# Moving the ALiBi bias of half of the heads behind exp, onto GpSimd, with a new order of the steps

## The chip, the core and the metric

The kernel runs on one core of a Trainium2 chip. A core has a matrix engine (TensorE, "PE" in the profile, with its weight loads as "PEld"), three engines for elementwise work (VectorE or "DVE", ScalarE or "ACT", GpSimd or "POOL"), and a queue that mostly issues transfers (SyncE, "SP"). Each engine works through its own list of instructions in order and waits for the others through semaphores. The metric is the device time of one execution in microseconds (us): the median over several executions.

## The reference

All data are fp32. The input is four batches of 1024 tokens with 128 features. Two blocks follow one another, and each adds to x the product of an attention and a gated feed-forward net:

```python
xn = layernorm(x);  x = x + attention_0(xn) * silu(ffn_0(xn))
xn = layernorm(x);  x = x + attention_1(xn) * silu(ffn_1(xn))
```

The first attention has 16 heads of 8 features, a causal window of 65 keys and a bias that falls linearly with the distance (ALiBi):

```python
score = q @ k.T / sqrt(128) + slope[head] * (key_pos - query_pos)
score = where((dist >= 0) & (dist <= 64), score, -inf)
out   = softmax(score) @ v
```

The first feed-forward net mixes eight experts' weights into one pair of matrices per batch, by gates that come from the mean over the batch's tokens. The second attention runs over the *batch* axis: each token position is a sequence of four. The second feed-forward net is silu(w1 x) * (w2 x), two square 512 by 512 layers with gelu, and a last projection.

## The kernel before

**Units and slices.** The first attention and all feed-forward work go by units: a unit is 512 tokens of one batch, and there are eight (0 to 7). Within a unit the first attention goes by four tiles of 128 queries (t = 0 to 3). The second attention goes by eight slices of 128 positions over all four batches; slices 0 to 3 need only units 0, 2, 4 and 5, slices 4 to 7 need all.

**The order is written out by hand.** `ORDER` is a list of words, each of them one step, and `program` emits the instructions of each word in that order (line 855). Every engine thus has its part of the list as its queue, and an instruction that waits holds up all that is behind it on its engine. `program` is emitted twice, with `exact` False and True, and a flag that the kernel computes from the weights (line 256) chooses one of them at run time. With these inputs the branch with `exact` False runs. The words that matter here, with u for the unit, t for the tile and b for the batch:

| word | step | engines |
|---|---|---|
| q u, m u g, v u i | queries, keys and values of a unit; copies with masks; copies of v | PE; ACT; DVE (ACT for unit 0) |
| s u t | `scores`: 12 matmuls into a tile `ps_S` of four PSUM banks, of which there is one (line 425) | PE |
| b u t | `biased`: score + bias from PSUM into an SBUF tile `pr` (line 442) | DVE |
| x u t | `power`: exp of `pr`, in place (line 776) | ACT |
| o u t | `weighted`: `pr` times v and a column of ones, so that the sums for the softmax come along (line 473) | PE |
| c, p, d | copy, transpose and divide by the sums | ACT, PE, DVE |
| A, B, C, D, E | gates of a batch and the mixing of experts, E being one of 16 adds (line 351) | PE, ACT, DVE |
| f, g | first net: gelu, then silu (lines 517, 532) | PE, ACT |
| r, l/t, n, k | residual; statistics, scaling and transposing back of a layernorm | POOL; DVE, POOL; DVE; PE, ACT |
| w, h, i, j | second net: gated, two square layers, last projection (lines 564, 576, 589) | PE, ACT, DVE |
| *A to *Y | second attention of one slice (lines 618 to 717): project, gates, products (*b), score (*C), exp (*E), norm (*N), values (*D), sums (*G), turn back (*T), project out (*F), output (*Y) | mostly DVE and POOL |
| y | last tokens of the last batch (line 731) | DVE |

The scores tile has one buffer, so s of the next tile can begin only when its readers are done. `pr` comes from a pool `big` of six tiles of 128x2048, which the nets and the second attention use too; in the first 40 us four of the six hold the experts' weights. The outputs of *Y and y go through `t2k`, a pool of three buffers, and are free again when their transfer has landed. PSUM tiles of one bank take turns over three banks, and `BANKS` writes out which.

**Bias and mask.** The array `bias` has, for each key (partition), head and query, the bias, and -1e30 where the mask forbids the key. It is loaded once (line 170) on ACT's queue, 1 MB. Heads lie in `bias[:, j, g]`, j and g from 0 to 3.

Of the kernel before, what the change touches and what calls it, by code (L numbers as in the profile page):

```python
# [11 lines left out]
AF = mybir.ActivationFunctionType  # L12
ALU = mybir.AluOpType
# [3 lines left out]
P = 128  # L17
# [29 lines left out]
def constants():  # L47
# [30 lines left out]


ORDER = """  # L80
    l1
    q0 m02 m00 m03 m01 A00 n10 s00 k10 b00 A01 B0 L0 s03 b03 C0 D0 E0 E0 E0 E0 v01 s01 b01 E0 H0 v03 E0 v02
    L1 x00 v00 E0 x01 E0 x03 s02 b02 E0 o00 o01 c01 E0 x02 f0 l3 E0 f0 f0 E0 o02 E0 o03 E0 E0 p01 E0 c03
    q1 d01 m13 g0 m12 m11 p03 l2 L2 d03 f0 m10 n20 g0 n30 k20 s10 b10 f1 r0 f1 f1 t0 f1 v12 A10 v13 n01 k30
    s13 b13 k01 A11 B1 w0 s11 v11 w0 w0 C1 l6 w0 b11 n60 x13 v10 x10 x11 h0 l4 g1 k60 s12 o10 n40 o11 c11 D1
    g1 b12 p11 E1 x12 h0 h0 d11 o12 l7 l5 o13 k40 c13 E1 E1 E1 E1 E1
    q2 E1 H1 m23 n50 v20 m21 m22 E1 v21 m20 h0 E1 s20 b20 f3 k50 E1 v23 A20 E1 f3 x20 p13 s22 d13 v22 r1 f2
    b22 t1 A21 x22 B2 i0 n11 n70 E1 E1 i0 s21 o20 b21 k11 x21 i0 C2 i0 D2 s23 o21 w1 b23 c21 w1 E1 w1 o22 w1
    x23 h1 p21 E1 f2 E1 o23 c23 Z f2
    q3 E2 f2 m31 m32 h1 m30 m33 E2 g2 v31 d21 E2 f3 E2 g2 p23 s30 d23 b30 f3 r2 x30 E2 v30 t2 h1 v33 h1 A30  # L90
    s31 E2 n21 v32 k70 j0 b31 x31 j0 E2 A31 o30 o31 E2 E2 c31 s32 f4 i1 b32 x32 s33 k21 b33 E2 x33 i1 f4 g3
    g3 p31 B3 o32 o33 H2 d31 E2 E2 c33 i1
    q4 E2 C3 v41 D3 w2 E3 m40 m41 m43 m42 p33 i1 s40 E3 d33 v40 r3 v43 w2 w2 w2 E3 b40 t3 x40 h2 h2 s41 v42
    E3 n31 h2 E2 b41 x41 h2 s42 o40 o41 k31 E2 z f4 b42 c41 f4 j1 j1 x42 s43 E3 b43 x43 i2 i2 w3 i2 w3 i2
    p41 o42 E2 o43 c43 w3
    q5 d41 v51 m50 w3 p43 m53 h3 g4 E3 m52 m51 g4 E3 h3 d43 h3 E3 v53 h3 s50 v52 b50 x50 i3 s51 f5 v50 i3
    b51 E3 j2 E3 r4 E3 f5 E3 E3 E3 x51 t4 i3 n41 s52 o50 o51 k41 b52 j2 w4 s53 w4 c51 w4 w4 H3 b53 x52 x53
    i3 h4 o52 o53 p51 f6 E3 c53 f6 d51
    q6 E3 f6 f5 p53 m60 f5 d53 f6 v63 j3 g6 v62 g5 v61 m62 g5 r5 t5 m61 j3 g6 n51 h4 h4 m63 k51 h4 s61 *A0
    i4 b61 *A0 s60 v60 w5 *A0 w5 w5 w5 x61 *A0 b60 x60 i4 i4 s62 *B0 *b0 i4 *A1 b62 *C0 h5 *E0 j4 o60 *N0  # L100
    o61 s63 c61 *D0 x62 j4 b63 h5 x63 *A1 h5 o62 o63 *A1 *A1 p61 c63
    q7 m70 d61 m73 p63 d63 v71 *B1 *D0 v72 *b1 m72 *G0 h5 f7 m71 i5 *A2 s70 r6 *A2 i5 b70 v73 x70 *C1 *E1
    v70 s71 *A2 *A2 b71 *N1 x71 i5 i5 *D1 o70 o71 s72 c71 f7 f7 b72 t6 f7 s73 x72 *D1 b73 n61 x73 g7 g7 j5
    p71 *B2 j5 k61 *b2 o72 d71 *G1 o73 c73 *A3 p73 d73 w6 *A3 *A3 r7 *A3 t7 w6 *C2 w6 *B3 *T0 w6 n71 *E2 h6
    *b3 *N2 *C3 k71 *D2 h6 *E3 h6 *N3 *D2 *D3 h6 w7 w7 *A4 *A4 *D3 w7 *A5 *A4 *G3 *A4 *A5 *B4 *A5 *A5 *b4
    *C4 *T3 i6 *B5 *T1 *F0 *E4 *b5 *C5 i6 i6 *E5 i6 *N4 *G2 j6 *Y0 *N5 j6 *D4 w7 *D4 *A6 *A6 *D5 h7 *G4 *A6
    *A6 *T2 *B6 *D5 *A7 *A7 *b6 *A7 h7 *F1 *C6 *E6 *A7 h7 *Y1 *G5 *B7 h7 *N6 *b7 *D6 *T5 i7 *C7 *E7 *D6 *N7
    *T4 *D7 *F5 i7 *G6 i7 *F3 *T6 *F2 *Y5 *F4 *D7 i7 *Y3 *G7 *T7 *Y4 *F6 *Y2 j7 *Y6 *F7 j7 y0 *Y7 y1
"""
# [10 lines left out]
def block_kernel(ctx: ExitStack, tc: tile.TileContext, a: dict, out: bass.AP):  # L122
    nc = tc.nc
    PE, DVE, ACT, POOL = nc.tensor, nc.vector, nc.scalar, nc.gpsimd
# [23 lines left out]
    g1 = main.tile([P, B, S], F32, tag="g1", name="g1")  # L148
# [18 lines left out]
    nc.scalar.dma_start(out=x[:, 0, U:S], in_=a["x"][:, U:S])  # L167
    nc.sync.dma_start(out=vec, in_=a["vec"])
    nc.sync.dma_start(out=wg, in_=a["wg"])
    nc.scalar.dma_start(out=bias.rearrange("p j g q -> p (j g q)"), in_=a["bias"])  # L170
    nc.sync.dma_start(out=tb.rearrange("p c e -> p (c e)"), in_=a["tb"])
    nc.sync.dma_start(out=w1, in_=a["w1"])
    nc.sync.dma_start(out=w2, in_=a["w2"])
# [113 lines left out]
    def program(exact):  # L287
# [8 lines left out]
        def big(shape=(P, 4, 4, P)):  # L296
            return ffn.tile(list(shape), F32, tag="big", name="big", bufs=6)
# [67 lines left out]
        made = {}  # L365
# [73 lines left out]

        def biased(u, t, sp):  # L440
            pr = big()
            DVE.tensor_tensor(pr, sp, bias, ALU.add)  # L442
# [153 lines left out]
        def attend(sl, pool, late):  # L596
# [110 lines left out]
            def gated_out():  # L707
# [63 lines left out]
        def bias_add(u, t):  # L771
            put(("pr", u, t), biased(u, t, made["sp", u, t]))

        def power(u, t):
            pr = made["pr", u, t]
            ACT.activation(pr, pr, AF.Exp)  # L776
# [158 lines left out]
```

## Time and profile before

| | us |
|---|---|
| median of 3 runs (lowest, highest) | 542.19 (541.60, 543.24) |
| the profiled execution | 542.32 |
| its span, first to last instruction | 540.5 |
| PE busy | 521.0 (96%) |
| DVE busy | 348.7 (65%) |
| ACT busy, of it table loads | 344.8 (64%), 127 |
| POOL busy | 119.7 (22%) |

The span and the profiled execution's own time differ by 1.8 us, which lie outside of the instructions. In the profile a matmul in fp32 appears as two instructions. A row of the groups gives the line, engine and operation, the tile written and those read, shapes and count, then the busy time in us and the mean in ns, then the idle time in front of it and what ended it.

### The profile page before, as it was taken

The page shows a single profiled execution, that of the slowest core. Times are in us where ns is not written, and L with a number is a line of the kernel's source. Part 1 is how long each engine was busy: PE and PEld are TensorE (multiplying, and loading weights), DVE is VectorE, ACT ScalarE, POOL GpSimd, SP SyncE. Part 2 cuts the span into 40 slices and gives each one's busy share as a digit, 9 for nine tenths or more (in the row PEclk, how much of TensorE's full clock was granted, in tenths as well). Part 3 has the DMA queues.
Part 4 walks back from the last instruction along what each step waited for, and adds up shares of the span by engine and source line. Part 5 has one row for each costly group of instructions (what it writes and reads, how often), then busy time and mean ns, then how long its engine had stood idle before and what let it go on. Part 6 is the DMA issues. An engine that isn't in the chain of part 4 may idle for free.

```text
span 540.5 us, 10505 instructions
## 1 busy us (share of the span) xinstructions
PE 521.0 (96%) x4448; PEld 293.3 (54%) x4448; DVE 348.7 (65%) x657; ACT 344.8 (64%) x417; POOL 119.7 (22%) x149
## 2 busy tenths in 40 slices
PE   8599999999999999999999999999999999999993
PEld 4266465545665545556455584446545744465453
DVE  6898778934563668114365223546578799888995
ACT  2477686976898766965596643557568565654441
POOL 3023011400210020000110002011142433737653
PEclk9889999999999999999999999999999999999998
DMA  8942005102221112011110000000000000000003
GB/s 318 403 182 99 2 2 158 54 26 79 79 79 41 41 40 79 1 40 39 40 40 2 1 1 0 1 0 3 1 1 3 1 0 1 0 20 2 19 15 108
DMA packets 10726, 27.32 MB, mean 51 GB/s; under 512 B 1040, under 2 KB 5296, under 8 KB 9648
## 3 DMA queue, kind: packets, MB, share of 16 engines
q1 hardware_dynamic: 10240, 25.01, 13.4%
q10 hardware_dynamic: 432, 1.57, 0.8%
q8 instruction: 36, 0.59, 0.4%
q14 instruction: 18, 0.15, 0.1%
HBM read 24.48 MB, written 2.10 MB: 49 GB/s over the span
## 4 chain that ended last, share of the span: by engine, by line
PE 83%; DVE 7%; DMA 4%; POOL 2%; issue 1%; ACT 1%; SPq 0%; DVEq 0%; POOLq 0%; ACTq 0%
PE ps_M L576 36%; PE ps_O L473 6%; PE ps_S L425 6%; PE ps_M L516 5%; PE ps_M L527 5%; PE ps_M L564 5%; PE ps_M L565 5%; PE ps_M L589 5%; PE ps_M L618 3%; DMA big<-in_tw 2%; DVE big L681 2%; DMA vec<-in_vec 1%; PE ps_M L231 1%; PE ps_V L390 1%; PE ps_S L387 1%; PE ps_S L388 1%
## 5 line engine op out<-in xcount | busy, mean ns | idle before, releaser
L576 PE MATMUL ps_M<-big,l1h 128*128 128x512 f32 x512 | 228.5, 594 | 1.1 <-ACT big L577 0.8
L576 PEld LDWEIGHTS ps_M<-big,l1h 128*128 128x128 f32 x512 | 95.0, 190 | 113.5 <-issue 104.7
L442 DVE TENSOR_TENSOR big<-ps_S,bias 128x2048 f32<-128x2048 f32 x32 | 73.2, 2288 | 32.3 <-PE ps_S L425 29.0
L577 ACT ACTIVATE big<-ps_M,vec 128x512 f32<-128x512 f32 x64 | 43.3, 687 | 53.6 <-PE ps_M L576 48.7
L776 ACT ACTIVATE big<-big 128x2048 f32<-128x2048 f32 x32 | 60.8, 1909 | 12.1 <-DVE big L442 11.7
L568 DVE SCALAR_TENSOR_TENSOR big<-ps_M,vec,t2k 128x512 f32<-128x512 f32 x32 | 23.9, 749 | 48.5 <-PE ps_M L565 26.1
L577 ACT ACT_TABLE_LOAD x36 | 46.2, 1283 | 3.2 <-PE ps_M L576 2.6
L537 POOL TENSOR_TENSOR g<-g,s 128x512 f32<-128x512 f32 x8 | 10.3, 1288 | 169.8 <-ACT g L532 80.5
L425 PE MATMUL ps_S<-qm,k 32*64 32x256 f32 (+1 forms) x768 | 37.2, 478 | 6.2 <-DVE big L442 6.2
L688 POOL TENSOR_TENSOR big<-big 128x512 f32<-128x512 f32 x16 | 21.8, 1363 | 68.5 <-DVE big L681 53.6
L473 PEld LDWEIGHTS ps_O<-big,vb 128*32 128x32 f32 x2048 | 30.6, 113 | 9.4 <-issue 7.3
L567 ACT ACTIVATE t2k<-ps_M,vec 128x512 f32<-128x512 f32 x32 | 21.9, 687 | 20.8 <-PE ps_M L564 20.4
L564 PE MATMUL ps_M<-xn,l1w 128*128 128x512 f32 x64 | 33.7, 609 | 0.2 <-ACT t2k L567 0.2
L473 PE MATMUL ps_O<-big,vb 128*32 128x64 f32 x2048 | 33.5, 224 | 0.0
L425 PEld LDWEIGHTS ps_S<-qm,k 32*64 32x64 f32 x768 | 18.9, 133 | 26.5 <-issue 9.0
L565 PE MATMUL ps_M<-xn,l1w 128*128 128x512 f32 x64 | 32.9, 595 | 0.2 <-ACT t2k L567 0.2
L516 PE MATMUL ps_M<-xn,mw 128*128 128x512 f32 x64 | 31.8, 607 | 0.0
L527 PEld LDWEIGHTS ps_M<-mw,big 128*128 128x128 f32 x256 | 30.0, 192 | 3.4 <-issue 2.9
L589 PEld LDWEIGHTS ps_M<-l1w,big 128*128 128x128 f32 x256 | 30.0, 192 | 3.4 <-issue 2.3
L351 DVE SCALAR_TENSOR_TENSOR mw<-tw,gr,mw 128x512 f32<-128x512 f32 x42 | 31.3, 746 | 0.7
L589 PE MATMUL ps_M<-l1w,big 128*128 128x128 f32 x256 | 30.9, 276 | 0.4 <-DVE t2k L714 0.4
L527 PE MATMUL ps_M<-mw,big 128*128 128x128 f32 x256 | 30.7, 276 | 0.0
(162 smaller groups left out, 702.7 us busy)
## 6 DMA issues: line engine op xcount, KB each, us to landing
tw<-in_tw SPq DMA_DIRECT2D x24, 512.0 KB, 3.9
big<-in_tw SPq DMA_DIRECT2D x4, 1024.0 KB, 9.0
l1h<-in_l1h SPq DMA_DIRECT2D x2, 1024.0 KB, 6.1
bias<-in_bias ACTq DMA_DIRECT2D x1, 1024.0 KB, 7.7
x<-in_x SPq DMA_DIRECT2D x1, 1024.0 KB, 5.0
out<-t2k SPq DMA_DIRECT2D x4, 256.0 KB, 2.8
l1w<-in_l1w SPq DMA_DIRECT2D x3, 256.0 KB, 5.2
out<-t2k SPq DMA_DIRECT2D x4, 192.0 KB, 2.1
```

Of the source, the lines that this page charges most:

```text
L351: DVE.scalar_tensor_tensor(m, more[e // 2][:, e % 2, :], gr[:, e:e + 1], base if e == 0 else m, ALU.mult, ALU.add)
L425: PE.matmul(sp[rows, j, :, q0:q0 + n], lhsT=k[r, key:key + W], rhs=qm[r, :, t * P + q0:t * P + q0 + n], start=True, stop=True,)
L442: DVE.tensor_tensor(pr, sp, bias, ALU.add)
L473: PE.matmul(op[32 * j:32 * j + 32, part, qs], lhsT=vb[:, col:col + 32], rhs=pr[:, j, g, qs], start=(odd + i + g == 0), stop=(odd + i + g = ...
L516: PE.matmul(hp, lhsT=m1[:, c * P:(c + 1) * P], rhs=xn[:, b, cx], start=True, stop=True)
L527: PE.matmul(op[:, i, :], lhsT=hid[:, c, i * P:(i + 1) * P], rhs=m2[:, c * D:(c + 1) * D], start=(c + i == 0), stop=(c + i == FC + 2))
L564: PE.matmul(p1, lhsT=wt["w1"][:, c * P:(c + 1) * P], rhs=xn[:, b, cx], start=True, stop=True)
L565: PE.matmul(p2, lhsT=wt["w2"][:, c * P:(c + 1) * P], rhs=xn[:, b, cx], start=True, stop=True)
L576: PE.matmul(hp, lhsT=wt[name][:, i, c * P:(c + 1) * P], rhs=hid[:, i, :], start=(i == 0), stop=(i == FC - 1))
L577: ACT.activation(new[:, c, :], hp, AF.Gelu, scale=v(name + "s", c))
L589: PE.matmul(op[:, k, :], lhsT=hid[:, i, at0:at0 + P], rhs=wt["w3"][:, i, :], start=(i + k == 0), stop=(i + k == FC + n - 2))
L776: ACT.activation(pr, pr, AF.Exp)
```

## The change

For heads with j = 0 and 1 the bias is no longer added to the score ahead of exp. exp is taken of the bare score, straight from PSUM, and GpSimd multiplies the result by exp(bias), which the host computes (it is 0 where the mask forbids a key). Heads with j = 2 and 3 keep the add. All this is for the branch with `exact` False; the other branch first loads the plain bias of j = 0 and 1. The load of the bias is cut into two of 512 KB on the same queue, of which the one for j = 2 and 3 goes first.

`ORDER` is a new permutation of the same 676 words, and `BANKS` fits it. The list below has its head, its first unit and its end.

```diff
-    nc.scalar.dma_start(out=bias.rearrange("p j g q -> p (j g q)"), in_=a["bias"])
+    nc.scalar.dma_start(out=bias[:, 2:4].rearrange("p j g q -> p (j g q)"), in_=a["bias"][:, 8 * P:])
+    nc.scalar.dma_start(out=bias[:, 0:2].rearrange("p j g q -> p (j g q)"), in_=a["factor"])
...
         def biased(u, t, sp):
             pr = big()
-            DVE.tensor_tensor(pr, sp, bias, ALU.add)
-            if exact:
+            if not exact:
+                DVE.tensor_tensor(pr[:, 2:4], sp[:, 2:4], bias[:, 2:4], ALU.add)
+            else:
+                DVE.tensor_tensor(pr, sp, bias, ALU.add)
                 if UNITS[u][1] == 0 and t == 0:
...
         def power(u, t):
             pr = made["pr", u, t]
-            ACT.activation(pr, pr, AF.Exp)
+            if exact:
+                ACT.activation(pr, pr, AF.Exp)
+            else:
+                ACT.activation(pr[:, 0:2], made["sp", u, t][:, 0:2], AF.Exp)
+                POOL.tensor_tensor(pr[:, 0:2], pr[:, 0:2], bias[:, 0:2], ALU.mult)
+                ACT.activation(pr[:, 2:4], pr[:, 2:4], AF.Exp)
...
         banks["next"] = iter(BANKS[BEGIN:])
+        if exact:
+            nc.scalar.dma_start(out=bias[:, 0:2].rearrange("p j g q -> p (j g q)"), in_=a["bias"][:, 0:8 * P])
...
         "bias": bias,
+        "factor": np.exp(bias[:, 0:8 * P]),
```

```diff
-    l1
-    q0 m02 m00 m03 m01 A00 n10 s00 k10 b00 A01 B0 L0 s03 b03 C0 D0 E0 E0 E0 E0 v01 s01 b01 E0 H0 v03 E0 v02
-    L1 x00 v00 E0 x01 E0 x03 s02 b02 E0 o00 o01 c01 E0 x02 f0 l3 E0 f0 f0 E0 o02 E0 o03 E0 E0 p01 E0 c03
-    q1 d01 m13 g0 m12 m11 p03 l2 L2 d03 f0 m10 n20 g0 n30 k20 s10 b10 f1 r0 f1 f1 t0 f1 v12 A10 v13 n01 k30
...
-    p71 *B2 j5 k61 *b2 o72 d71 *G1 o73 c73 *A3 p73 d73 w6 *A3 *A3 r7 *A3 t7 w6 *C2 w6 *B3 *T0 w6 n71 *E2 h6
-    *b3 *N2 *C3 k71 *D2 h6 *E3 h6 *N3 *D2 *D3 h6 w7 w7 *A4 *A4 *D3 w7 *A5 *A4 *G3 *A4 *A5 *B4 *A5 *A5 *b4
-    *C4 *T3 i6 *B5 *T1 *F0 *E4 *b5 *C5 i6 i6 *E5 i6 *N4 *G2 j6 *Y0 *N5 j6 *D4 w7 *D4 *A6 *A6 *D5 h7 *G4 *A6
-    *A6 *T2 *B6 *D5 *A7 *A7 *b6 *A7 h7 *F1 *C6 *E6 *A7 h7 *Y1 *G5 *B7 h7 *N6 *b7 *D6 *T5 i7 *C7 *E7 *D6 *N7
-    *T4 *D7 *F5 i7 *G6 i7 *F3 *T6 *F2 *Y5 *F4 *D7 i7 *Y3 *G7 *T7 *Y4 *F6 *Y2 j7 *Y6 *F7 j7 y0 *Y7 y1
+    l1 n10
+    q0 m00 m03 m02 m01 k10 A00 A01 B0 s00 b00 C0 D0 E0 v03 E0 E0 E0 x00 s01 v00 b01 x01 v02 E0 E0 v01 l2 s02
+    b02 x02 E0 L0 E0 o00 s03 b03 E0 x03 o01 c01 E0 H0 L1 n20 E0 f0 f0 E0 E0 E0 f0 o02 o03 f1 k20 E0 f0 E0 p01
+    E0 c03
+    q1 m11 l3 d01 m13 g0 m10 v11 v13 m12 g0 p03 d03 n30 f1 r0 L2 s10 k30 v12 f1 A10 A11 Z t0 f1 b10 g1 B1
+    x10 n01 C1 k01 D1 g1 v10 s11 l7 E1 w0 E1 w0 w0 b11 n70 w0 E1 x11 h0 s12 o10 b12 l4 E1 x12 o11 h0 s13 l6
...
+    c71 b73 *C2 w6 w6 j5 x73 *E2 j5 *A3 *N2 *D2 *B3 p71 o72 d71 o73 c73 w6 *b3 w6 p73 d73 h6 *C3 *T0 r7 t7
+    h6 *E3 h6 *D2 *N3 h6 *D3 n71 k71 *D3 *A4 *A4 *A5 *F1 *G2 *Y1 w7 *A5 *A4 *G3 *A5 *A4 *A5 *T3 *B4 *b4 w7
+    w7 *C4 w7 i6 *F0 *B5 h7 *b5 *E4 *C5 *Y0 *E5 i6 i6 *N5 i6 *N4 *D5 *D4 *D5 *T2 *D4 h7 *A6 *A6 *A6 *G5 *A7
+    *A6 *B6 *A7 *b6 *A7 *T5 *C6 h7 *E6 *G4 *N6 *A7 *D6 *B7 j6 *b7 *F5 *D6 h7 j6 *C7 i7 *E7 *Y5 *N7 *T4 i7 i7
+    *G6 *T6 *D7 *F2 *F4 *F3 *D7 *Y2 *G7 i7 *T7 *Y4 *F6 *Y3 *Y6 j7 y0 *F7 j7 *Y7 y1
```

More of the change, by code (lines that the diff above doesn't have):

```diff
@@ L80 @@
 ORDER = """
-    l1
-    q0 m02 m00 m03 m01 A00 n10 s00 k10 b00 A01 B0 L0 s03 b03 C0 D0 E0 E0 E0 E0 v01 s01 b01 E0 H0 v03 E0 v02
-    L1 x00 v00 E0 x01 E0 x03 s02 b02 E0 o00 o01 c01 E0 x02 f0 l3 E0 f0 f0 E0 o02 E0 o03 E0 E0 p01 E0 c03
-    q1 d01 m13 g0 m12 m11 p03 l2 L2 d03 f0 m10 n20 g0 n30 k20 s10 b10 f1 r0 f1 f1 t0 f1 v12 A10 v13 n01 k30
-    s13 b13 k01 A11 B1 w0 s11 v11 w0 w0 C1 l6 w0 b11 n60 x13 v10 x10 x11 h0 l4 g1 k60 s12 o10 n40 o11 c11 D1
-    g1 b12 p11 E1 x12 h0 h0 d11 o12 l7 l5 o13 k40 c13 E1 E1 E1 E1 E1
@@ L87 @@
[L87 to L103, printed above, removed]
-    p71 *B2 j5 k61 *b2 o72 d71 *G1 o73 c73 *A3 p73 d73 w6 *A3 *A3 r7 *A3 t7 w6 *C2 w6 *B3 *T0 w6 n71 *E2 h6
@@ new lines @@
+    b02 x02 E0 L0 E0 o00 s03 b03 E0 x03 o01 c01 H0 L1 n20 E0 f0 f0 E0 E0 E0 f0 o02 o03 f1 k20 E0 f0 E0 p01
+    E0 c03
+    q1 m11 l3 d01 m13 g0 m10 v11 v13 m12 g0 p03 d03 n30 f1 r0 L2 s10 k30 v12 f1 A10 A11 Z t0 f1 b10 g1 B1
+    x10 n01 C1 k01 D1 g1 v10 s11 l7 E1 w0 E1 w0 w0 b11 n70 w0 E1 x11 h0 s12 o10 b12 l4 E1 x12 o11 h0 s13 l6
+    b13 x13 E1 n40 E1 k70 c11 h0 h0 H1 n60 p11 o12 E1 o13 k40 c13 E1
+    q2 l5 v21 m22 m21 v20 m23 d11 m20 k60 i0 f2 s20 E1 v23 b20 E1 x20 i0 p13 d13 n50 r1 s21 b21 E1 x21 A20
@@ new lines @@
+    i0 i0 A21 v22 E1 t1 f2 s22 f3 k50 f2 b22 f3 x22 B2 C2 A30 A31 o20 o21 n11 s23 k11 E1 b23 x23 c21 j0 f3
+    j0 p21 E1 o22 E1 o23 d21 c23 w1
+    q3 m31 D2 w1 B3 w1 v30 E2 m33 E2 w1 m32 E1 m30 f3 h1 p23 f2 v33 E2 s30 d23 E2 v31 b30 E2 v32 C3 x30 E2
+    E2 h1 g2 E2 g3 s31 b31 D3 x31 g2 h1 h1 s32 o30 E2 r2 o31 b32 x32 E2 t2 c31 f4 g3 E2 s33 b33 x33 i1 i1 f4
+    n21 o32 o33 p31 k21 d31 c33
+    q4 m43 i1 w2 E2 i1 j1 m42 v42 p33 d33 j1 m40 r3 v43 v41 E3 v40 w2 m41 w2 s40 w2 b40 x40 h2 h2 E3 t3 E2
@@ new lines @@
+    s41 b41 x41 H2 f4 h2 s42 o40 b42 o41 x42 h2 i2 E3 s43 E3 z b43 E3 i2 f6 c41 x43 i2 p41 d41 i2 o42 n31 E2
+    o43 E3 c43 E2
+    q5 k31 j2 E3 E3 v50 E2 j2 m52 w3 w3 m50 m53 w3 m51 w3 v52 h3 g4 f4 s50 E3 v51 b50 p43 x50 E3 d43 h3 v53
+    H3 s51 E3 b51 E3 g4 r4 x51 h3 h3 o50 o51 s52 t4 E3 E3 n41 b52 x52 i3 k41 c51 i3 p51 f5 s53 d51 o52 b53
+    w4 w4 w4 x53 i3 i3 f5 f7 o53 c53 f5 w4 E3 f5
+    q6 f7 f6 f6 m63 v62 E3 m62 v63 f7 p53 m60 d53 m61 g5 g5 r5 s60 t5 n51 g6 f6 j3 g6 b60 v61 j3 h4 k51 *A0
@@ new lines @@
+    *A0 *A0 *A0 h4 *B0 *b0 *A1 *C0 x60 h4 h4 s61 v60 w5 b61 i4 x61 *E0 i4 i4 *A1 w5 o60 o61 s62 c61 b62 w5
+    x62 *A1 i4 j4 *N0 j4 w5 p61 h5 s63 b63 x63 h5 d61 *A1 o62 o63 c63 *B1 *b1
+    q7 f7 *D0 m70 *D0 m71 h5 v72 *A2 m72 m73 *A2 h5 *C1 p63 *E1 d63 s71 v70 r6 b71 *A2 *N1 *D1 x71 g7 i5 *D1
+    *A2 t6 v71 s70 g7 b70 i5 *G1 x70 v73 *T1 n61 i5 s72 b72 k61 *B2 i5 x72 *b2 *G0 *A3 *A3 *A3 o70 o71 s73
+    c71 b73 *C2 w6 w6 j5 x73 *E2 j5 *A3 *N2 *D2 *B3 p71 o72 d71 o73 c73 w6 *b3 w6 p73 d73 h6 *C3 *T0 r7 t7
@@ L114 @@
 BANKS = (
-    "0120120120102102102102021021021021021021021012012012012012012021021012012020210120120120120121012012"
-    "0120120120120120120120120201202012012010102102102102102102102110210210210210210210210210210210210210"
-    "210210210120120120120101201201202102102102102102021021021021021020120120121021"
+    "0120120120120120120120120120120121201201201201202120120210210210201201012012012012012012120120120120"
+    "1021021021021021020120120120120101102102102102102102102102102012102102102102102102102102102120120120"
+    "120201201201201021020120120120120120120120120120120210210210210210212012012012"
 )
```

## The prediction

> **What bounds the kernel now.** I read the page first, then PE's waits, stretches of time, and the timelines of both ends.
>
> ```profile
> span 540.5 us, 10505 instructions
> PE 521.0 (96%) x4448; PEld 293.3 (54%) x4448; DVE 348.7 (65%) x657; ACT 344.8 (64%) x417; POOL 119.7 (22%) x149
> PE 83%; DVE 7%; DMA 4%; POOL 2%; issue 1%; ACT 1%; SPq 0%; DVEq 0%; POOLq 0%; ACTq 0%
> L442 DVE TENSOR_TENSOR big<-ps_S,bias 128x2048 f32<-128x2048 f32 x32 | 73.2, 2288 | 32.3 <-PE ps_S L425 29.0
> L776 ACT ACTIVATE big<-big 128x2048 f32<-128x2048 f32 x32 | 60.8, 1909 | 12.1 <-DVE big L442 11.7
> L688 POOL TENSOR_TENSOR big<-big 128x512 f32<-128x512 f32 x16 | 21.8, 1363 | 68.5 <-DVE big L681 53.6
> ```
>
> PE is busy for 521.0 of 540.5 us and carries 83% of the chain; 19.5 us are idle. The add that the change halves mostly waits for PE (29.0 us). Where does PE idle? The stretches (length, then PE's busy time first):
>
> ```profile
> 18.00:22.00 4.00, 1.78 (x42) 1.15 (x41) 3.07 (x9) 3.94 (x7) 0.00 (x0) 1.00 0.99 402
> 22.00:26.00 4.00, 1.83 (x22) 0.78 (x6) 3.79 (x6) 0.57 (x1) 0.00 (x0) 0.50 1.01 392
> 100.00:150.00 50.00, 50.00 (x465) 26.84 (x464) 26.82 (x59) 39.03 (x43) 6.24 (x8) 1.00 0.17 54
> 530.00:540.50 10.50, 2.76 (x25) 2.57 (x23) 5.18 (x7) 0.77 (x2) 2.95 (x3) 0.85 0.31 98
> ```
>
> From 50 to 450 us PE idles 0.2 us. The rest is the head (9 us before 30 us, partly at a clock of 0.5), 1 us from 450 to 485, 1.5 us from 485 to 530, and 7.7 us at the end. So in the middle a faster DVE is worth nothing; only the two ends can gain, and the middle can only lose.
>
> In the head DVE holds PE up, as PE's longest waits show:
>
> ```profile
> PE ps_S L425 <- DVE big L442: 6.2, 3, 3.8
> ```
>
> The fourth scores run at 27.64, when the third add (25.30 to 27.6) is done, which is behind four expert adds (E) of 0.75.
>
> At the end DVE and PE finish almost together. DVE is done with n71 at 440.6 and with its last y at 536.9; PE takes up k71 at 440.9 and ends at 532.8. The last outputs then wait for a buffer:
>
> ```profile
> 534.83 0.56 DVE L715 TENSOR_TENSOR t2k<-xn,g 128x384 f32<-128x384 f32 x1 [1.65 <-DMA out<-t2k]
> ```
>
> **What the Trainium skill says.** "GPSIMD Engine Reference", section 1 (Specifications): POOL's SBUF interfaces are shared with VectorE, in contention with DVE instructions in a 2-port mode or with two SBUF inputs. The trace agrees: four values products (L681, two SBUF inputs) take 3.55 us instead of 4 x 0.65 = 2.6 just when a POOL add runs, and that takes 1.65 instead of 1.27.
>
> ```profile
> 452.77 1.65 POOL L688 TENSOR_TENSOR big<-big 128x512 f32<-128x512 f32 x1 [1.56 <-DVE big L681]
> 451.41 3.55 DVE L681 TENSOR_TENSOR big<-av,apr 128x512 f32<-128x512 f32 x4
> ```
>
> DVE thus lost 0.95 of 1.65 us. By the same rule the bias add has one SBUF input (the other is PSUM) and should not collide, the E adds with two should. "ScalarE: Activation LUTs", "What ACT_TABLE_LOAD costs": 1283 ns for each change of set, and an ACTIVATE of N elements takes a fixed part plus 0.833 N ns. The trace has 1283 ns, and 1909 for N = 2048.
>
> **The change part by part**, against the profiled execution's span (540.5; its time is 542.32, and the median 542.19 is 0.1 below that).
>
> *Removed:* half of each add. From 2288 for 2048 and 0.833 x 1.25 = 1.04 ns per element (1243 ns for the 1024-wide L657, 2288 for 2048), a half takes 1.22 us. DVE saves 32 x 1.07 = 34 us, 30 of them in the middle under PE, worth nothing there.
>
> *Added on ACT:* exp in two halves. 1.91 - 1024 x 0.833 = 1.06 us each at most, so +0.2 us per tile or 6 us. Counting the changes of function along the list of words gives 99 loads for the old order, as in the trace from 36+19+15+9+7+7+6, and 108 for the new: +9 x 1.28 = 11.5 us. ACT goes from 345 to some 362. Its densest stage is q2 of the new order: 38 us of work and loads to 40 us of PE (old q3: 44 to 50). It is covered by PE as long as ACT is not late.
>
> *Added on POOL:* 32 products of 128x1024. The free minimum at 128x512 is 1.27 us (L688), so 2 x 1.27 = 2.5 us, 81 in all; POOL goes from 120 to 200 us, 37%. Bounds: 2.3 us if the fixed part is shared, 3.3 if each is stretched as L688's worst (1.65). For a tile the way from scores to `pr` was 2.29 + 1.91 = 4.2 us; now it is 1.06 + 2.5 = 3.6 on one side and 1.22 + 1.0 on the other. Behind the product on POOL wait layernorm's rstd and the residual; their readers n and t come several us later.
>
> *New wait:* s of the next tile must wait for ACT's first half too, not only for DVE. What is behind s on PE is everything. In the new order x always stands ahead of the next s, with PE work between them. At s21 that is 3.8 us (i0, p13) against a table load and a half exp (1.28 + 1.06): covered. At s11 PE has 6.1 us (k30, f1, A10, A11, f1, g1, k01, g1), ACT 7.3 (0.6 + 0.7 + 1.3 + 1.8 + 0.7 + 1.3 + 1.06): some 1 us of stall. I take +1 us for the middle; bounds 0 and 4 (a tenth of a us at each of 32 tiles, and 1).
>
> *Moved, head:* n10 now stands ahead of q0, so DVE's k (12.52) comes behind n10 (to 14.8), and s00 also behind A01: 16.8 instead of 14.17. But then only one half add stands before C0, and the first E comes at about 20.0 instead of 22.08. Gain 2 us, if nothing collides: the experts' first tile has landed by 14.2. But POOL's products of x00 (about 19.4 to 21.9), x01 (22 to 24.6) and x02 lie on E0s, and by 0.95 of 1.65 DVE loses 0.6 of each overlap: 2.5 x 0.6 = 1.5 us per product, two of them before the third add, 3 us, against 2 + 1.07 gained. The fourth scores move to about 30, but o00 is now ahead of them and PE has done about as much by 37.5 us as before. I take -0.5; bounds -2 and +5.9 (four products wholly on top, 10.2 - 4.3). The split load has the same bytes and one more issue of 0.45 us on ACT (1.62 to 2.07 for the old one), ahead of a table load whose user waits until 9.57: nothing. Without that cover 0.45.
>
> *Moved, tail:* the list now does all of h6, and D2, before k71. From n71 on DVE had 90.8 us of work by the rows' means and took 96.3 (+5.5). In the new list it has w 4 x 0.75, *A 16 x 0.45, *b 4 x 2.45, *C 4 x 4.1, *N 4 x 1.64, *D 9 x 1.5, *G 6 x 0.69, *Y 8 x 1.6 and y 2 x 1.5: 76.4. PE had 87.0 behind k71 (88.9 busy); now 12 x 3.44 (i, h), 4 x 1.72, 4 x 1.78, 16 x 0.70, 6 x 0.44, 8 x 0.89: 76.2. PE's total is unchanged, so it reaches k71 later by 10.8 x 1.02 = 11.0, at 451.9. DVE then ends at 451.9 + 76.4 + 5.5 = 533.8, the span 3.6 later (as from 536.9 to 540.5): 537.4. By PE: 452.4 + 77.7 + 2.5 idle = 532.6, then silu 0.4, y 1.5 and 3.6: 538.1. So the later one, -2.4. What the tail gains is the wait for `t2k` and DVE's backlog behind PE.
>
> Sum: 540.5 - 0.5 + 1 - 2.4 = 538.6, and with 1.8 around it 540.4.
>
> **The rivals.** *New waits eat the gain:* s behind ACT costs 0.1 us at most tiles, or DVE's stall in the tail is 8 and not 5.5: +2, 542.4. For it: ACT's 108 loads; against: the old middle lets PE idle for 0.2 us at ACT loads as dense.
>
> *POOL takes DVE's port in the head (slower):* products and E0s exclude each other in full. Then DVE's expert adds, from 20 us, are late by 5.9, f0 with them, and PE idles at a clock of 0.5: -0.5 becomes +4.5 on average of 3 and 5.9, the time 545.4. It decides from about 6 us of overlap in the first 36 (6 x 0.6 + 1 = 4.3 saved). For it: 16 x 0.75 = 12 us of E0 and 10 of products within 18 us. Against: DVE's half adds and statistics (7 us) don't collide, and POOL runs there.
>
> *DVE is the true bound at both ends:* head -2, middle 0, tail -2.4 and the t2k wait gone (-0.8 more): 537.1. For it: DVE's 97% between 485 and 530; against: the collisions seen there.
>
> That the change does nothing is excluded by the branch that runs.
>
> **How the numbers follow.** Chances: small gain 0.45 (540.4), waits 0.20 (542.4), slower 0.25 (545.4), full gain 0.10 (537.1). A change of 0.3% (1.6 us) is about the least that measurements of this kernel can tell. Of the first case two thirds to three quarters lie below 540.6 (0.33), the rest within; of the second 0.02, 0.12 and 0.06; the others on their sides. Faster 0.45, same 0.24, slower 0.31. The range is 537.0 to 546.0; it leaves out a tenth at each end. The likeliest case alone: 539 to 542.
>
> **What would show it.** The half adds at 1.22, halves of exp near 1.05, products near 2.5 and POOL near 200 us; 108 table loads; the first E0 near 20 us, and E0s of 1.5 to 2 us where a product runs; PE's idle time from 50 to 450 at about 1 us with ACT's exp as releaser; k71 near 452. I am wrong if PE idles by more than 3 us in the middle, if PE has done visibly less by 38 us, or if the last DVE work ends later than 536.

## The result, and the profile after

The changed kernel takes 556.21 us (median of 4, 554.87 to 558.45) against 542.40 of the kernel before beside it: a ratio of 1.0256, with a 95% interval of 1.0232 to 1.0280. It is 13.8 us slower; the prediction said 540.4, and at most 546. The profiled execution took 555.42 us.

The page of the kernel after, in the order in which the kernel before was shown: the span, the busy times, the chain's shares, and the groups of the half addition, of the exponential from PSUM and of the product.

```profile
span 553.4 us, 10596 instructions
...
PE 523.0 (95%) x4448; PEld 294.1 (53%) x4448; DVE 346.1 (63%) x657; ACT 357.9 (65%) x458; POOL 199.5 (36%) x181
...
PE 77%; DVE 12%; POOL 3%; DMA 3%; ACT 3%; issue 2%; SPq 0%; ACTq 0%; DVEq 0%; POOLq 0%
...
L786 POOL TENSOR_TENSOR big<-big,bias 128x1024 f32<-128x1024 f32 x32 | 77.1, 2411 | 196.4 <-ACT big L785 181.4
...
L447 DVE TENSOR_TENSOR big<-ps_S,bias 128x1024 f32<-128x1024 f32 x32 | 39.1, 1221 | 53.3 <-PE ps_S L428 47.9
...
L785 ACT ACTIVATE big<-ps_S 128x1024 f32<-128x1024 f32 x32 | 32.8, 1024 | 13.3 <-DVE big L447 12.9
```

Two things stand out. VectorE's additions fell by 34.1 us (73.2 to 39.1), but its busy time only by 2.6 (348.7 to 346.1), so some 31 us came back in other rows: the normalisations nt, four in each step n (L222), went from 355 to 546 ns on average, and the expert sums E on streamed weights (L354) from 746 to 866. And the exponential, which was to run beside the addition, waits for the addition.

TensorE's time by stretch in the kernel after (length, busy time, granted clock, share of the DMA engines, GB/s):

```profile
0.00:40.00 40.00, 28.59 (x350) 0.83 0.76 280
40.00:60.00 20.00, 17.74 (x175) 1.00 0.33 116
60.00:450.00 390.00, 386.68 (x3611) 1.00 0.09 30
450.00:545.50 95.50, 90.03 (x331) 1.00 0.05 16
```

The same stretches of the kernel before (the last one ends at 532.8) give 30.96, 20.00, 389.80 and 80.25 us of busy time. TensorE's last instruction ends at 545.3. So it idles more by 2.4 us in the head, 2.3 between 40 and 60, 3.1 in the middle and 2.7 from 450 on, 10.5 in all; its busy time is 2.0 us longer, with a mean clock of 0.83 in place of 0.87 in the head, where the half clock lasts until about 36 us and not 32; and the end behind it is 0.4 us longer (8.1 against 7.7). That is the span's 12.9 us. TensorE's waits name what it stood for:

```profile
PE ps_S L428 <- ACT big L785: 8.0, 3, 5.7
PE ps_M L234 <- DVE nt L222: 3.5, 5, 1.0
```

In the head it now waits for ACT's first exponential and not for VectorE's addition. The normalisations nt are second, with 3.5 us in 5 waits, where the kernel before had 0.4 in one.

The timeline of the kernel after around 20 us, of all engines:

```profile
20.24 0.75 DVE L354 SCALAR_TENSOR_TENSOR mw<-big,gr,w 128x512 f32<-128x512 f32 x1
...
20.78 2.42 POOL L786 TENSOR_TENSOR big<-big,bias 128x1024 f32<-128x1024 f32 x1 [6.58 <-issue]
21.02 4.30 DVE L354 SCALAR_TENSOR_TENSOR mw<-big,gr,mw 128x512 f32<-128x512 f32 x3
...
25.24 1.22 DVE L447 TENSOR_TENSOR big<-ps_S,bias 128x1024 f32<-128x1024 f32 x1
...
26.49 1.02 ACT L785 ACTIVATE big<-ps_S 128x1024 f32<-128x1024 f32 x1 [4.44 <-DVE big L447]
...
27.57 1.16 PE L428 MATMUL ps_S<-qm,k 32*64 32x512 f32 x8 [5.75 <-ACT big L785]
```

This is the head's loss in one chain. The first E starts where it was forecast, at 20.24. Then the product starts on GpSimd at 20.78, and the three E behind it take 4.30 us where three took 2.33 before: one of them stood until the product ended at 23.20. The second half addition comes at 25.24, when the kernel before was already at its third whole one (25.30); the exponential waits for its end, at 26.46, and only then can TensorE write the third scores, at 27.57, after 5.75 us. The fourth follow at 32.09 (27.64 before).

The last output waits for a buffer as before:

```profile
547.89 0.56 DVE L721 TENSOR_TENSOR t2k<-xn,g 128x384 f32<-128x384 f32 x1 [2.45 <-DMA out<-t2k]
```

### The profile page after: what moved, and what is told of

Its sections match the earlier page's. It is cut to its first block, busy times and chain, and to the rows that moved or that the text cites. A ratio compares the mean times of both kernels' runs of the same rounds, so it can differ in the third digit from the quotient of the medians.

```text
span 553.4 us, 10596 instructions
## 1 busy us (share of the span) xinstructions
PE 523.0 (95%) x4448; PEld 294.1 (53%) x4448; DVE 346.1 (63%) x657; ACT 357.9 (65%) x458; POOL 199.5 (36%) x181
## 4 chain that ended last, share of the span: by engine, by line
PE 77%; DVE 12%; POOL 3%; DMA 3%; ACT 3%; issue 2%; SPq 0%; ACTq 0%; DVEq 0%; POOLq 0%
PE ps_M L582 31%; PE ps_S L428 6%; PE ps_O L479 5%; PE ps_M L533 5%; PE ps_M L570 5%; PE ps_M L522 5%; PE ps_M L571 5%; PE ps_M L595 4%; PE ps_M L624 3%; DVE big L687 2%; DVE nt L222 2%; PE ps_M L234 1%; PE ps_S L390 1%; PE ps_V L393 1%; PE ps_S L391 1%
## 5 line engine op out<-in xcount | busy, mean ns | idle before, releaser
L786 POOL TENSOR_TENSOR big<-big,bias 128x1024 f32<-128x1024 f32 x32 | 77.1, 2411 | 196.4 <-ACT big L785 181.4
L447 DVE TENSOR_TENSOR big<-ps_S,bias 128x1024 f32<-128x1024 f32 x32 | 39.1, 1221 | 53.3 <-PE ps_S L428 47.9
L583 ACT ACT_TABLE_LOAD x38 | 48.8, 1283 | 13.4 <-PE ps_M L582 12.8
L785 ACT ACT_TABLE_LOAD x26 | 33.4, 1283 | 13.3 <-DVE big L447 12.9
L785 ACT ACTIVATE big<-ps_S 128x1024 f32<-128x1024 f32 x32 | 32.8, 1024 | 13.3 <-DVE big L447 12.9
L354 DVE SCALAR_TENSOR_TENSOR mw<-tw,gr,mw 128x512 f32<-128x512 f32 x42 | 36.2, 866 | 1.2 <-DMA tw<-in_tw 0.8
L222 DVE TENSOR_SCALAR nt<-x,mv,rstd 128x128 f32<-128x128 f32 x64 | 30.8, 546 | 5.0 <-POOL rstd L217 4.9
L787 ACT ACTIVATE big<-big 128x1024 f32<-128x1024 f32 x32 | 33.6, 1049 | 0.0
L694 POOL TENSOR_TENSOR big<-big 128x512 f32<-128x512 f32 x16 | 23.8, 1491 | 23.6 <-DVE big L687 23.5
```

The source lines that it names most:

```text
L222: DVE.tensor_scalar(nt[:, i, :], src[:, i, :], mv[:, i, 0:1], rstd[:, i:i + 1], ALU.subtract, ALU.mult)
L447: DVE.tensor_tensor(pr[:, 2:4], sp[:, 2:4], bias[:, 2:4], ALU.add)
L583: ACT.activation(new[:, c, :], hp, AF.Gelu, scale=v(name + "s", c))
L785: ACT.activation(pr[:, 0:2], made["sp", u, t][:, 0:2], AF.Exp)
L786: POOL.tensor_tensor(pr[:, 0:2], pr[:, 0:2], bias[:, 0:2], ALU.mult)
```

## The experiments

Each kernel ran on the same chip as a kernel before beside it. Times are medians; "over before" is against that kernel before (541.9 to 542.4 in the six sets). The ratio and its 95% interval are taken over the runs, so the ratio is not exactly that of the medians.

| kernel | us | over before | ratio, interval |
|---|---|---|---|
| the change | 556.21 | +13.8 | 1.0256, 1.0232 to 1.0280 |
| order_only | 558.82 | +16.7 | 1.0307, 1.0290 to 1.0324 |
| ops_only | 593.22 | +51.1 | 1.0936, 1.0909 to 1.0964 |
| no_product | 549.05 | +6.9 | 1.0117, 1.0081 to 1.0153 |
| split | 554.09 | +12.0 | 1.0237, 1.0203 to 1.0272 |
| split_no_product | 548.25 | +6.3 | 1.0111, 1.0086 to 1.0135 |
| n30_early | 552.58 | +10.6 | 1.0195, 1.0178 to 1.0212 |
| tail_spread | 554.64 | +12.7 | 1.0237, 1.0194 to 1.0280 |
| head_plain | 555.47 | +13.5 | 1.0253, 1.0236 to 1.0270 |
| side_product | 554.11 | +12.2 | 1.0209, 1.0180 to 1.0239 |
| one_input | 552.09 | +10.2 | 1.0178, 1.0160 to 1.0195 |
| all_three | 550.32 | +8.4 | 1.0153, 1.0136 to 1.0171 |
| all_three_np | 544.89 | +3.0 | 1.0049, 1.0036 to 1.0063 |
| all_four | 553.13 | +10.8 | 1.0198, 1.0179 to 1.0217 |
| all_four_np | 547.42 | +5.1 | 1.0088, 1.0067 to 1.0109 |
| all_four_b | 548.70 | +6.5 | 1.0115, 1.0098 to 1.0132 |
| four_b_head_np | 544.06 | +2.0 | 1.0031, 1.0023 to 1.0040 |
| all_four_b_np | 542.67 | +0.4 | 1.0009, 1.0002 to 1.0016 |
| before_split | 543.18 | +0.8 | 1.0015, 0.9998 to 1.0033 |

### The parts, one at a time

order_only is the kernel before with the new `ORDER` and `BANKS` alone. (The list of the new order above shows one E0 too many: in the kernel H0 follows c01 directly, and there are 16 E0 as before.)

> The new order of steps and banks with the old operations (one add of all heads on DVE, one exp, no product on GpSimd). Theory P (the product on GpSimd holds the SBUF interface that DVE needs) and theory W (the first half of exp waits for the add and holds the scores' tile longer): the order alone is harmless, 540 to 545 us. Theory O (the new order is itself worse, in head and tail): most of the 13.8 us remain, 550 us or more.

It is slower than the whole change. The full addition (2.29 us) stands in the new head, which was laid out for the half one; TensorE waits 3.95 us for the second addition there, where the change waits 5.75 us behind the product. From 60 to 450 us it idles 5.1 us against the change's 3.3, and near the end it waits 3.5 us for the value sums (L694 there) against 2.4. So the new order isn't harmless and doesn't stand alone: it is bound to the new operations. That doesn't say what part of the change's 13.8 us is the order's.

ops_only is the reverse, the new operations in the old order, with the first exponential put right behind the half addition (the cut shows this move against the change, with the function that each line stands in):

```diff
-                ACT.activation(pr[:, 0:2], made["sp", u, t][:, 0:2], AF.Exp)     (in power)
+                ACT.activation(pr[:, 0:2], sp[:, 0:2], AF.Exp)                   (in biased)
```

> The changed operations in the old order of steps and banks; the first half of exp stands right behind the add on ACT, since the old order has later scores ahead of exp. Theory P and W: as slow as the changed kernel or slower, 553 to 562 us, since the order does not fit the new operations. Theory O: within 4 us of before, 546 us or less.

Its 593 us are no measure of the operations: the exponential is now at the place of step b in ACT's queue, and TensorE waits 16.3 us for it and 11.6 in the two largest waits for other work of ACT. The two runs together show only that order and operations can't be judged apart by exchanging them whole. I went on by mending one suspected stall at a time.

no_product leaves GpSimd's product out (half of the heads without bias and mask):

```diff
-                POOL.tensor_tensor(pr[:, 0:2], pr[:, 0:2], bias[:, 0:2], ALU.mult)
```

> The changed kernel without the product on GpSimd: half of the heads go without bias and mask, all else stays. Theory P: the expert adds fall back to 0.75 us each, at least 6 of the 13.8 us come back, 545 to 550 us. Theories W and O: less than 3 us come back, 553 us or more; ACT still waits some 26 us for the add in front of the first half of exp.

The product is worth about 7 us, half of the loss. The other half remains with it gone. Without the product no E takes longer than 753 ns, so the long E all go with it. A mark for the head is the time at which TensorE starts q1, the queries of unit 1: 43.46 us in the change, 40.88 here. In the profiles, then, 2.6 us of the product's cost have arisen by there.

split gives the scores two tiles of PSUM, so that exponential and addition read different tiles (the products for q and k of units 1 to 7, which shared the old tile, go to the first of the two):

```diff
-            sp = four((P, 4, 4, P))
+            sp = two(0), two(1)
...
-                DVE.tensor_tensor(pr[:, 2:4], sp[:, 2:4], bias[:, 2:4], ALU.add)
+                DVE.tensor_tensor(pr[:, 2:4], sp[1], bias[:, 2:4], ALU.add)
...
-                ACT.activation(pr[:, 0:2], made["sp", u, t][:, 0:2], AF.Exp)
+                ACT.activation(pr[:, 0:2], made["sp", u, t][0], AF.Exp)
```

> The changed kernel with the scores in two PSUM tiles of two banks each in place of one of four, so that the first half of exp waits for PE alone and runs beside the add. Theory W: ACT's 26 us of waiting for the add vanish, PE's 8 us of waiting for ACT at the scores fall below 3, 546 to 551 us. Theory P: DVE's stalls behind the product stay, 553 us or more. Theory O: 554 us or more.

With one tile the exponential waits for the addition's end (12.9 us of ACT's idle time are put down to it, and as much before its table loads); with two it starts at 18.38 while the addition runs from 18.18. So the two readers were put one behind the other because they read one tile, 1.22 + 1.02 us in series. The stalls at 114 and 116 us (1.8 us) go too, as they do in no_product. The time falls by some 2 us, but its interval overlaps the change's, so a gain is not shown. In the head nothing is won by it alone: the 5.7 us wait becomes one of 5.1 for the addition.

split_no_product leaves both out.

> Both suspects out together: the scores of heads 0 and 1 and of heads 2 and 3 in two tiles of PSUM, so that the first exponential runs beside the addition, and GpSimd's products left out (half of the heads go without bias and mask). If the product (7 us, from the run without it) and the serial wait (2 us, from the run with split scores) add up, 547 us; if the serial wait only showed where a product followed it, 549 as without the product alone. Either way it stays above the kernel before, 542, by what the order of the steps itself costs; 542 or less would say that the order costs nothing.

548.25: hardly less than without the product alone (549.05), with overlapping intervals. So in the total no cost of the serial reading by itself is shown, with or without the product. And 6.3 us remain.

### How the product acts

side_product keeps GpSimd as busy, on the same inputs, but nobody waits for what it writes; one_input keeps the wait, but GpSimd reads one tile instead of two. In both, half of the heads go without bias and mask.

```diff
-                POOL.tensor_tensor(pr[:, 0:2], pr[:, 0:2], bias[:, 0:2], ALU.mult)
+                POOL.tensor_tensor(bias[:, 0:2], pr[:, 0:2], bias[:, 0:2], ALU.subtract)    (side_product)
+                POOL.tensor_scalar(pr[:, 0:2], pr[:, 0:2], 1.0, None, ALU.mult)             (one_input)
```

> The changed kernel with GpSimd's multiplication turned into a subtraction of the same two inputs and size, whose result goes over the factor's tile and not into the scores (half of the heads go without bias and mask). GpSimd is busy as before, in the same places, but no matrix product waits for it. If the product's 7 us come from the chain exponential, product, weighted sums, about 549 us as without the product. If they come from what GpSimd's work does to VectorE and to its own queue, 555 to 556 as in the changed kernel.

> The changed kernel with GpSimd's multiplication by the factor turned into one by the number 1: one input in SBUF in place of two, in the same place and with the same waits (half of the heads go without bias and mask). If VectorE is held up only while GpSimd reads two inputs, VectorE's busy time falls from 346 to near 325 us and the time to 549 to 551. If any long GpSimd instruction holds it up, VectorE stays near 346 or in proportion to the instruction's length, and the time at 554 to 556.

Taking the wait for the product away gives 2.1 us by the medians, with overlapping intervals; VectorE is busy for 342.2 us, nearly as long as in the change (346.1). Taking the second input away gives 4.1 us, with intervals apart, and that although the instruction is longer; VectorE's busy time falls to 329.5 us, of 324.7 without the product. The minimum, median and maximum of E and of GpSimd's instruction in the kernel after (ns, and the time of the first and last):

```profile
L786 POOL TENSOR_TENSOR big<-big,bias x32: 2344/2363/2806, 20.8 to 439.0; 128x1024 f32<-128x1024 f32 x32
...
L354 DVE SCALAR_TENSOR_TENSOR mw<-tw,gr,mw x42: 718/743/2727, 67.2 to 315.5; 128x512 f32<-128x512 f32 x42
```

and in one_input:

```profile
L786 POOL TENSOR_SCALAR big<-big x32: 2766/2782/3214, 20.5 to 436.9; 128x1024 f32<-128x1024 f32 x32
...
L354 DVE SCALAR_TENSOR_TENSOR mw<-tw,gr,mw x42: 716/743/1406, 67.2 to 313.1; 128x512 f32<-128x512 f32 x42
```

An E that meets a product of two inputs is late by up to 1.98 us (2727 less 743). One that meets a GpSimd instruction of one input, 2.78 us long, is late by 0.66 at most, and the head of one_input shows when:

```profile
20.47 2.83 POOL L786 TENSOR_SCALAR big<-big 128x1024 f32<-128x1024 f32 x1 [6.61 <-ACT big L785]
20.69 2.98 DVE L354 SCALAR_TENSOR_TENSOR mw<-big,gr,mw 128x512 f32<-128x512 f32 x3
```

The three E take 0.65 us more than 2.33 together, and are nearly done when the GpSimd instruction ends at 23.30. So VectorE is held up by the instruction that GpSimd runs beside it, and not through a dependency or by GpSimd's load as such. That the number of inputs makes the difference is likely but not shown: the two GpSimd instructions also differ in kind (TENSOR_TENSOR and TENSOR_SCALAR). "SBUF — State Buffer", section "SBUF: two separate sides", has it as an exclusive lock on a shared pair of ports that one side holds for the whole instruction, while the other is blocked fully. The trace agrees for the product. For GpSimd's one-input form, which reads SBUF too, a wait of 0.66 in 2.78 us is less than the page says.

head_plain keeps the old addition and exponential in the first unit alone, with no product there (the factor is loaded later, over the bias of its heads).

> The changed kernel, but the first unit of attention one keeps the full addition and one exponential over four heads, with no product; all other units have the change. Port theory for the head: the second to fourth E of the second sequence fall back from 4.3 us to 2.2, the third scores start some 2 us sooner, and the kernel takes 552 to 554. If the head's loss is only the order of the steps there, the time stays at 556.

555.47: not to be told from the change. The E are short again, but the full addition of 2.29 us is back in front of each scores tile: the second wait for an addition becomes 3.94 us, and q1 starts at 43.25 us, against 43.46 in the change and 40.88 without the product. In this head the half addition is worth about as much as the product costs.

### Stalls of the order

n30_early moves one word.

```diff
-    v11 v13 m12 g0 p03 d03 n30 f1 r0
+    v11 v13 n30 m12 g0 p03 d03 f1 r0
```

> The changed kernel with one step moved in its order: the bank's tokens n30 go ahead of g0, p03 and d03, so that its four transpositions run on VectorE before GpSimd starts the residual r0 and the averages of Z. Port theory (a VectorE instruction with two inputs or a two-port form waits for a running GpSimd instruction): the three idle pieces of TensorE at 52 to 55 us, 2.25 us in sum, go, and the kernel takes about 554 us, 2 less than the changed kernel. If those pieces come from the depth of the queue alone and not from GpSimd, they stay or move and the time is 556 as before.

3.6 us less than the change (3.2 by the table's column), with intervals apart. The timeline of the kernel after at that place:

```profile
51.19 3.97 DVE L222 TENSOR_SCALAR nt<-x,mv,rstd 128x128 f32<-128x128 f32 x4
...
51.42 1.27 POOL L543 TENSOR_TENSOR g<-g,s 128x512 f32<-128x512 f32 x1 [2.71 <-DVE s L513]
...
52.76 1.26 POOL L544 TENSOR_TENSOR x<-x,g 128x512 f32<-128x512 f32 x1
...
53.99 1.09 POOL L850 TENSOR_TENSOR l1w<-l1w,vec 128x512 f32<-128x512 f32 x1
54.17 0.33 PE L234 MATMUL ps_M<-cst,nt 128*128 128x128 f32 x1 [1.02 <-DVE nt L222]
```

and in n30_early:

```profile
49.15 1.11 DVE L222 TENSOR_SCALAR nt<-x,mv,rstd 128x128 f32<-128x128 f32 x4
```

Four instructions of 0.34 us take 3.97: they stand until GpSimd's three end, one after the other, and TensorE waits in between. (nt reads only one full tile from SBUF, so this form is held up too.) GpSimd's work here is not the product but the residual and Z, which scales the weights of the last projection (L850), as in the kernel before; the new order had put n30 on top of them. This part of the loss isn't the product's at all.

The idle pieces were 2.25 us, the gain 3.6. A half-clock stretch can follow a stall of that size. In no_product, which has the same stall, the granted clock (third number from the end) is:

```profile
52.00:53.00 1.00, 0.36 (x2) 0.80 0.00 0
53.00:54.00 1.00, 1.00 (x3) 0.50 0.37 61
...
55.00:56.00 1.00, 1.00 (x2) 0.50 0.95 401
56.00:57.00 1.00, 1.00 (x3) 0.99 0.99 401
```

3.4 us at half speed (52.6 to 56.0); in order_only it was 6.8 us (54.7 to 61.5), in the profiled execution of the change none. "TensorE: Matmul & The Clock Gate", Part 1, gives some 3.4 us as the time that a return to the full clock takes; the stretch in no_product agrees, and that in order_only is twice as long. That it is sometimes there and sometimes not would also explain why the change's own runs differ by 3.6 us, but that is not shown.

tail_spread takes the four last *D steps apart.

```diff
-    *D5 *D4 *D5 *T2 *D4 h7 *A6 *A6 *A6 *G5 *A7
+    *D5 *A6 *D4 *A6 *D5 *T2 *A6 h7 *D4 *G5 *A7
```

> The changed kernel with its last steps in another order: *D5 *A6 *D4 *A6 *D5 *T2 *A6 h7 *D4 *G5 *A7, where the four *D steps (whose residual sums and value additions run on GpSimd) no longer follow each other. If the clump of *D steps with GpSimd's additions is what costs the end 3.7 us (idle pieces of 1.31 at 502 and 2.40 at 530), 1 to 2 us go and the time is 554 to 555. If the end is set by the backlog that comes from before 460 us, nothing goes: 556.

1.6 us less, within the spread (551.6 to 556.1): by itself undecided. One idle piece at 502 us went from 1.31 to 0.59, the last from 2.40 to 2.25.

### Together

all_three has split, n30_early and tail_spread; all_three_np the same without the product.

> The changed kernel with three mends together: scores in two tiles of PSUM, n30 ahead of g0, p03 and d03, and the last *D steps spread. Single gains were 2.1, 3.6 and 1.6 us. If they add up, 549; if each only uncovers the next stall, 552 or more.

> The same three mends and no product on GpSimd (half of the heads go without bias and mask). If the order's own cost is in those named stalls, 548.2 less 3.6 and 1.6: 543, the time of the kernel before. If the order costs elsewhere, at 335, 461 and 502 us, in the half-clock stretch of the head, 545 to 547.

550.3 and 544.9: 5.4 us of the change's 13.8 are these three mends' (apart, by the same column, 1.8, 3.2 and 1.1, or 6.1), and 3.0 remain without the product. The idle pieces pointed to n71 near 452 us, 0.72 and 0.84, with a stretch near half clock behind them in all_three_np (0.53 and 0.61 between 454 and 458). all_four and all_four_np move n71 behind w7 and ahead of the value products.

```diff
-    h6 *D3 n71 k71 *D3 *A4 *A4 *A5 *F1 *G2 *Y1 w7
+    h6 w7 n71 *D3 k71 *D3 *A4 *A4 *A5 *F1 *G2 *Y1
```

> The changed kernel with the three mends and a fourth: n71 behind w7 and ahead of the value products. If the stall at n71 (1.57 us, and a half-clock stretch that can follow) goes, 548 to 549; if it only moves, 550 as with three mends. Faster than the kernel before is expected by neither theory.

> The same four mends and no product on GpSimd (half of the heads go without bias and mask). If the rest of the order's cost lies in the stall at n71 and its half clock, 542.5 to 543.5; if it lies elsewhere, 545 as with three mends.

A miss: 553.1 and 547.4, worse by 2.4 and 2.1 us by the column. VectorE's timeline in all_four_np tells why:

```profile
455.00 0.75 DVE L578 SCALAR_TENSOR_TENSOR big<-ps_M,vec,t2k 128x512 f32<-128x512 f32 x1 [3.76 <-ACT t2k L577]
455.66 1.11 DVE L225 TENSOR_SCALAR nt<-x,mv,rstd 128x128 f32<-128x128 f32 x4
```

w7 brought its gated product along, which waits 3.76 us for ACT's SiLU, and n71's four instructions stand behind it in VectorE's queue. I had moved the step for its matrix products and not counted what else it issues. all_four_b and all_four_b_np move n71 alone.

```diff
-    h6 *D3 n71 k71 *D3
+    h6 n71 *D3 k71 *D3
```

> The changed kernel with three mends and n71 ahead of both *D3 steps, w7 as in the changed kernel. If the second piece of the stall (0.84 us, VectorE's value products ahead of n71's instructions) goes and with it a half-clock stretch, 548 to 549.5; if nothing comes of it, 550.3 as with three mends.

> The same and no product on GpSimd (half of the heads go without bias and mask). 543 to 544 if the stall at n71 accounts for a part of the order's 3 us; 545 if not.

548.7 and 542.67. Without the product, the mended order is within 0.1% of the kernel before. So the order's loss is accounted for: its remaining 3 us lay mostly at n71. With the product 6.0 us are left. The head of all_four_b, and then of all_four_b_np, on VectorE and at TensorE's start of q1:

```profile
22.45 4.29 DVE L357 SCALAR_TENSOR_TENSOR mw<-big,gr,mw 128x512 f32<-128x512 f32 x3
26.65 1.22 DVE L450 TENSOR_TENSOR big<-ps_Sb,bias 128x1024 f32<-128x1024 f32 x1
...
44.38 1.02 PE L393 MATMUL ps_Sa<-xn,wqkv 128*128 128x512 f32 x2
```

```profile
20.74 2.33 DVE L357 SCALAR_TENSOR_TENSOR mw<-big,gr,mw 128x512 f32<-128x512 f32 x3
22.99 1.22 DVE L450 TENSOR_TENSOR big<-ps_Sb,bias 128x1024 f32<-128x1024 f32 x1
...
39.80 1.02 PE L393 MATMUL ps_Sa<-xn,wqkv 128*128 128x512 f32 x2
```

The two kernels differ in the product alone: with it the second half addition starts 3.66 us later and q1 4.6 us later. With one tile of scores q1 lost only 2.6 us. With two, the first two products follow each other without a gap (19.35 to 24.61), and the first also catches a small addition ahead of the E (1.97 us instead of 0.16). four_b_head_np leaves out the four products of the first unit alone.

```diff
-                POOL.tensor_tensor(pr[:, 0:2], pr[:, 0:2], bias[:, 0:2], ALU.mult)
+                if u:
+                    POOL.tensor_tensor(pr[:, 0:2], pr[:, 0:2], bias[:, 0:2], ALU.mult)
```

> The changed kernel with four mends (scores in two tiles, n30, the last *D steps, n71) and without the product in the first unit alone: its four tiles go without bias and mask in half of the heads, the other 28 products stay. If the product's cost lies in the head, where the traces of the two kernels with four mends differ by 4.5 us of idle time before 40 us, 543 to 544.5. If it is spread over the 32 tiles, 548.

544.06. Four of the 32 products cost 4.6 us, the other 28 together 1.4. The loss of 13.8 us then reads: 5.4 for the three mends (serial reading, n30, the last *D), 1.9 for n71, 4.6 for the products in the head, 1.4 to 1.5 for the other products, 0.4 left. The parts came off in this order; in another the shares differ, as the two marks for q1 show (2.6 and 4.6 us for the head's products).

before_split is the kernel before, in its own order, with the scores in two tiles and the addition in two halves of 1.22 us.

> The kernel before, in its own order, with nothing of the change but the scores in two tiles of PSUM and the bias added in two halves. The matrix products of the next scores can follow the first half's addition (1.22 us) and needn't wait for the whole (2.29 us). If the tile of scores is what binds the head, its two idle pieces (2.22 and 3.81 us) shorten by about 1 us each and the time is 540 to 541, under the kernel before. If VectorE's extra 32 times 0.15 us and the order of its queue take it back, 542 as before.

543.18, not faster. The head's second wait falls from 2.22 to 1.05 us, the third only from 3.81 to 3.58, since the addition there is held up by four E and not by its own length; and TensorE is busy 2.9 us longer, though this kernel takes the same matrix products. Where that comes from stays open. No kernel of the table beats the kernel before.

## Why the prediction was wrong

**Sizes** were right: half additions 1221 ns (1.22 forecast), exponentials 1024 and 1049 (1.05), products 2411 (2.5), GpSimd 199.5 us (200), ACT 358 (362), nine more table loads, first E at 20.24 (20.0). None of that decided. (The 1283 ns for a change of set are the table load alone. The page cited for it counts a drain of some 1380 ns on top; in the changed kernel the loads at 115.13 and 118.37 us start within 0.02 us of the end of the instruction in front, and ACT goes on within 0.02 us of their ends, so no such drain shows.) The median was 10 us above the range's end because three steps failed, all in one direction.

**Moved, head (-0.5).** The overlap's price failed. From one collision in the kernel before (0.95 of 1.65 us) I took 0.6 of each overlap; it is nearly the whole rest of the GpSimd instruction (an E of 2.73 us, where 1.5 to 2 were named). I also let two products cost 3 us against 3.07 gained, and didn't follow the late addition into the next scores and into the half clock. Measured: the head's products cost 2.6 us until q1 in the change, and 4.6 us in all with two tiles of scores. The rival "POOL takes DVE's port in the head" had this mechanism and nearly its size (3 to 5.9); it got a chance of 0.25. The argument against it, that half additions and statistics don't collide, is true (1206 to 1225 ns for all 32 half additions), but the E stand between them in the queue.

**New wait (+1).** "1.06 + 2.5 on one side and 1.22 + 1.0 on the other" failed: the two sides are in series, 1.22 + 1.02 + 2.41, since two engines reading one tile of PSUM were put one behind the other. The stall forecast at s11 (1 us) did not come. 1.8 us came at 114 to 116, in unit 2, which the prediction took as covered "as long as ACT is not late": ACT had waited 3.61 us for a half addition there. Split took this away, and so did leaving out the product. The middle's other loss wasn't in any term: 2.25 us at n30, where VectorE's nt met GpSimd's residual and Z. "In the middle a faster DVE is worth nothing" was right; that a few slower instructions of VectorE could stop TensorE there was not asked.

**Moved, tail (-2.4).** The sums of VectorE's and TensorE's work could not see stalls that come from the order itself, and they dropped a wait. In the changed kernel k71's products begin at 464.33 us and not at 452.4, most of it inherited from the head and the middle. In all_four_b_np they begin at 452.36, as forecast, though that is luck (this kernel has no product and an order with mended stalls); so this run tests the tail's own part. TensorE there ends at 533.5 and not 532.6, and the last output still waits 1.43 us for `t2k`, a wait that the forecast took as gone (1.65 before, 2.45 in the change). These two, 0.9 and 1.4 us, make most of the difference of the span, 540.6 and not 538.1. VectorE's stalls were too small as well: behind n71 it takes 85.8 us in the change (464.1 to 549.9), 9.4 more than the 76.4 of the sum, where 5.5 was carried over; the rival "new waits" had 8. The gain of 2.4 doesn't exist.

**The signs of being wrong** all came: more than 3 us of idle time in the middle (5.6 from 50 to 450), less done in the head (TensorE busy for 2.4 us less by 40), the last work of VectorE at 549.9, later than 536. The range failed because each rival was one mechanism alone, and the range's end took in the worst of one; here three came together. The likeliest case took -0.5 for the head, well below the middle of its own bounds (-2 to +5.9).

## What to carry to other kernels

Work moved to GpSimd to relieve VectorE isn't free where VectorE has instructions that GpSimd holds up, here sums of two SBUF inputs and normalisations from SBUF: price each meeting at the whole rest of GpSimd's instruction, and look for it where VectorE's queue is what TensorE waits for, here mostly at the first 4 of 32 products. A new order can cause such meetings with old work of GpSimd too, as at n30. A one-input form on GpSimd, even a longer one, may do less harm. Before counting on two engines to read one PSUM tile side by side, look whether they do, and when a step is moved, follow every instruction that it issues through each queue.

## What the runs showed of the hardware that I had not expected

- A GpSimd multiplication with one input (2.78 us) held up VectorE's two-input sums by 0.66 us at most, one with two inputs (2.36 us) by 1.98.
- Small instructions are caught as well: an addition of 128x4 took 1.97 us in the head of all_four_b and 0.16 in all_four_b_np.
- A stall of TensorE of 2.3 us in pieces was followed by 3.4 us at half clock in one kernel, 6.8 in another and none in a third. Estimated from these, with half of the stretch lost, it cost between 2.3 and some 5.5 us.
